# VectorE and ScalarE in source order in the gated layers, W_down's sums two steps ahead, Silu on ScalarE

## The chip, the cores and the metric

The kernel runs on one core of one Trainium2 chip. The metric is the device time of one execution in microseconds (us). Before the change the median of three runs is 2498.24 us (2491.13 to 2501.68). All arithmetic is float32.

## What is computed

Four residual layers follow each other on x of shape 32 x 64 x 1024. Cut to what matters:

```python
x = x + conv(x)                                  # a long convolution along 1024, kernel from L0's states
x = x + einsum('bsi,boi->bso', x, W1[ids1])      # one 1024 x 1024 matrix per batch row, picked by an index
x = x + einsum('bij,bkj->bik', x, W2[ids2])      # the same again
def lora(base, inp, A, B):                       # rank 16, A and B picked per batch row
    t = einsum('bri,bni->bnr', A[ids], inp)
    return base + einsum('bor,bnr->bno', B[ids], t) * 0.5
gate = lora(einsum('bnh,fh->bnf', x, W_gate), x, A_gate, B_gate)    # F = 2752 hidden columns
up   = lora(einsum('bnh,fh->bnf', x, W_up),   x, A_up,   B_up)
act  = silu(gate) * up
x = x + lora(einsum('bnf,hf->bnh', act, W_down), act, A_down, B_down)
```

## The kernel before

**Chunks and stages.** The 32 batch rows form four chunks of eight (`NCK`, 512 columns of 64 positions each). The convolution comes first, for all chunks; its result for chunks 1 to 3 waits in DRAM (`cd`). Then chunk 0's two picked matrices are applied, row by row, as sixteen "adapters": `adapter` (L275) multiplies eight 512 KB weight tiles with x, and VectorE transposes the sum and adds it (L285, L287). From there on each chunk runs `ffn`, and the adapters of the next chunk are put between its steps, where DMA loads would otherwise be few: the generator `others`, taken one at a time by `other()`.

**The gated layers.** 2560 of the hidden columns are worked through in five groups (`gi`), in three blocks: group 0, groups 1 and 2, groups 3 and 4. `gated` makes the gate product, applies Sigmoid on ScalarE and a multiplication on VectorE (L680, L681), makes the up product and multiplies (L685). The left-over columns are `rest`, three products of 7 us, in the first block. After each block W_down's product for that block is made, in steps of two column tiles, for four values of `h`.

**Fewer products by sums.** All large products use a scheme with seven products in place of eight, in which both operands are first added and subtracted (`sides`, `stationary` L430 to L433 for weights, `moving` L447 to L450 for activations) and the seven products are added afterwards. Chunk 0 (`halves`) uses one level of it, computes the weights' sums, and also stores those of a second level in DRAM (`kept`, `kept_parts`). Chunks 1 to 3 (`quarters`) use two levels and load stored sums. One `quarters` call is four `unit`s: unit (0), then (5,6), (4,3) and (1,2). In a unit TensorE makes products 0, 5, 6, 4, 1 and then two more into banks `pa`, `pb`, `pc`, `pd`; ScalarE copies `u` and `v` out (L623, L625, L635) and VectorE adds (L629, L631, L633, L639). In a unit of two, `pd` is the same bank as `pb`, and product 2 goes into it a second time, so that it waits for L633; product 3 goes into `pc` and waits for L631.

**Buffers.** All weight tiles, of adapters, gate, up and W_down, and the four tiles of stored convolution that each chunk takes over, share one ring of nine slots (`wpool`, tag "w"), filled by SP's queue in a fixed order. The sums of the weights have two slots, `up` and Sigmoid's output share one (tag "cu").[...]

**What sets the order.** TensorE's order is that of the source (`manual_schedule`). On the other engines a scheduler sets it, by priorities and estimated times, when the kernel is built; `behind(last_add)` and `behind(last_copy)` tie some work to stand behind a named instruction on its engine. Each engine then runs its list in order. W_down's step loads two tiles, makes four sums and multiplies:

```python
with behind(last_add):
    ws = stationary(wt, nt, s_tile(gpool, f"{name}_{s0}"))
for j in (0, 5, 6, 4, 1, 3, 2):
    terms = [(ws[j][:, i, :], ab[s0 - m0 + i][j]) for i in range(nt)]
```

`between(i)` is called at the end of each gate and up product: from the third on it takes an adapter, before that it brings the next chunk's x and stored convolution (`bring`) and adds the latter (`take`, L238). `moving_of(c + 1)` makes the next chunk's moving operands in the last block, all at h = 1.

Of the kernel before, what the change touches and what calls it, by code (L numbers as in the profile page):

```python
# [13 lines left out]
SP = mybir.EngineType.SP  # L14
POOL = mybir.EngineType.Pool

P = 128
# [3 lines left out]
NCK = 4  # L21
# [49 lines left out]
def kernel(  # L71
# [139 lines left out]
    last_add, last_copy = [], []  # L211

    def behind(last):
        return tc.issue_after(last[-1]) if last else ExitStack()


# [16 lines left out]
    def take(c, quarters):  # L233
        n = H // 4
        for q in quarters:
            xv = xs[c].rearrange("p k (b h) -> p (k b) h", h=H)[:, :, q * n : (q + 1) * n]
            with tc.issue_after(last_add[-1]):
                nc.vector.tensor_add(xv, xv, came.pop(q).rearrange("p i k -> p k i"))  # L238


# [56 lines left out]

    hpool = ctx.enter_context(tc.tile_pool(name="hpool", bufs=1, reuse_waits="tile"))
# [30 lines left out]
    def columns(table, c, n, name):  # L329
# [17 lines left out]
        def in_order():  # L347
            t = gpool.tile([P, n, BC, R], F32, tag="at", name=f"at_{name}", bufs=1)
            with behind(last_copy):
                nc.scalar.copy(t, raw.rearrange("p b n r -> p n b r"))  # L350
            return t.rearrange("p n b r -> p n (b r)")
# [111 lines left out]
    def halves(c, gi, g, o, xb, between):  # L463
        name = f"{c}_{gi}_{g}"
        w = (wg, wu)[g]
        lt, copy_lt = low_rank_of(c, gi, g)
        wts, sts, sides_of = [], [], []
        for m in range(MG):
            wt = []
            for i in (0, 1):  # L470
                t = wpool.tile([P, 2, KH, P], F32, tag="w", name=f"wf{i}_{name}_{m}")
                nc.sync.dma_start(t.rearrange("p k s f -> p (k s f)"), w[i, MG * gi + m])
                wt.append(t)
            wts.append(wt)

        def stationary_of(m):
            st = s_tile((gpool, qpool[0])[m], f"{name}_{m}")
            sts.append(st)
            with behind(last_add):
                sides_of.append(stationary(wts[m], KH, st))  # L480

        stationary_of(0)

        def kept(q):
# [12 lines left out]
            with behind(last_add):  # L497
                sides(a11, a12, a21, a22, *(t[:, :n, i] for i in range(4)))
# [18 lines left out]
        for m in range(MG):  # L517
# [25 lines left out]
            last_copy.append(nc.scalar.copy(v, pb).ins)  # L543
            if m == 0:
                with behind(last_copy):
                    copy_lt()
            last_add.append(nc.vector.tensor_add(u, v, u).ins)
            if m == 0:
                stationary_of(1)
                kept_parts()  # L550
            product(pc, 6, True)
            nc.vector.tensor_add(c22, pc, u)
            product(pb, 4, True)
            last_add.append(nc.vector.tensor_add(c22, pb, c22).ins)
# [4 lines left out]
            nc.vector.tensor_add(c12, pb, u)  # L559
            product(pc, 3, False)  # L560
            last_add.append(nc.vector.tensor_add(c21, pc, u).ins)
            kept(2 * m + 1)
            o_m = o[:, :, m]
            with behind(last_add):
                nc.vector.tensor_add(o_m, o_m, lt[:, :, m])
        between()

    def quarters(c, gi, g, o, xb, between):
# [26 lines left out]
        def unit(js, copies=None):  # L595
# [18 lines left out]
            banks = [ps_tile(f"pq{i}_{name}_{js_}")[:, : n * TQ] for i in range(5 - n)]  # L614
            pa, pb, pc, pd = (banks + banks[1:2])[:4]
# [5 lines left out]
            )  # L621
            product(pa, 0, True)
            nc.scalar.copy(u, pa)  # L623
            product(pb, 5, True)
            last_copy.append(nc.scalar.copy(v, pb).ins)  # L625
            if copies:
                with behind(last_copy):
                    copies()
# [4 lines left out]
            nc.vector.tensor_add(c22, pd, c22)  # L633
            product(pa, 1, False)
            nc.scalar.copy(c11, pa)  # L635
            for i in (3, 2) if n == 1 else (2, 3):
                ps, to = ((pd, c12), (pc, c21))[i - 2]
                product(ps, i, False)
                nc.vector.tensor_add(to, ps, u)  # L639
# [16 lines left out]
        (p1,) = unit((0,), copy_lt)  # L656
        nc.scalar.copy(c12, p1)
        add(c11, p1, l11)
        p6, p7 = unit((5, 6))
        add(c12, c12, p6)  # L660
        add(c21, c12, p7)
        p5, p4 = unit((4, 3))
        add(c22, c21, p5)
        add(c12, c12, p5)
        add(c21, c21, p4)
        add(c12, c12, l12)
        add(o[:, 1], o[:, 1], lt[:, 1])  # L667
        p2, p3 = unit((1, 2))
        add(c11, c11, p2)
        last_add.append(add(c12, c12, p3).ins)  # L670
        between()

    def gated(c, gi, xb, between):

        f = quarters if c else halves
        act = apool.tile([P, 2, MG, TC], F32, tag="act", name=f"act_{c}_{gi}")
        f(c, gi, 0, act, xb, lambda: between(2 * gi))
        sg = gpool.tile([P, 2, MG, TC], F32, tag="cu", name=f"sg_{c}_{gi}", bufs=1)
        for i in (0, 1):
            nc.scalar.activation(sg[:, i], act[:, i], AF.Sigmoid)  # L680
            nc.vector.tensor_mul(act[:, i], act[:, i], sg[:, i])  # L681
        up = gpool.tile([P, 2, MG, TC], F32, tag="cu", name=f"up_{c}_{gi}", bufs=1)
        f(c, gi, 1, up, xb, lambda: between(2 * gi + 1))
        for i in (0, 1):
            nc.vector.tensor_mul(act[:, i], act[:, i], up[:, i])  # L685
        return act

    def rest(c):
# [3 lines left out]
        for i in range(3):  # L692
            wt = wpool.tile([P, KT, P], F32, tag="w", name=f"wr{i}_{c}")
            nc.sync.dma_start(wt.rearrange("p k f -> p (k f)"), wr[i])
            if i == 2:
# [6 lines left out]
                nc.scalar.activation(rest1, cs[0], AF.Sigmoid)  # L702
                nc.vector.tensor_mul(rest1, rest1, cs[0])
# [22 lines left out]
        nc.scalar.activation(a[SECOND], v[SECOND], AF.Sigmoid)  # L726
        nc.vector.tensor_mul(a[SECOND], a[SECOND], v[SECOND])
# [6 lines left out]
    def prepare(c, name):  # L734

        x_c = xs[c]
        at = columns(ag if name == "g" else au, c, KT, f"{name}_{c}")()
        ps = low_rank(at, KT, lambda i: x_c[:, i, :], f"{name}_{c}")
        nc.vector.tensor_mul(tms[name], ps, bmask)

    def moving_of(c):
# [25 lines left out]
        for i in (0, 1):  # L767
            b11, b12, b21, b22 = (q_of(k, t)[i] for k in (0, 1) for t in (0, 1))
            moving(b11, b12, b21, b22, *(at_(j)[i] for j in (4, 5, 6, 3)))
            for j, q in zip(range(3), (b11, b21, b22)):  # L770
                nc.scalar.copy(at_(j)[i], q)
        b11, b12, b21, b22, t1, t2, t4 = (xd[:, :, i] for i in range(7))
        moving(b11, b12, b21, b22, t1, t2, b12, t4)
        return xd

    def ffn(c, xb, others):

        x_c = xs[c]
        ready = None

        def other():
            next(others, None)

        def between(i):

            if i > 2:
                other()
            elif c + 1 < NCK:
                if i == 1:
                    take(c + 1, (0, 1))  # L790
                if i < 2:
                    bring(c + 1, (2 * i, 2 * i + 1))
# [5 lines left out]
        for block, (m0, m1) in enumerate(BLOCKS):  # L798
# [3 lines left out]
            acts = []  # L802
            for gi in range(m0 // MG, m1 // MG):
                acts.append(gated(c, gi, xb, between))
            for _ in left:
                pass
            at = at()
            if c == 0 and last:
# [3 lines left out]
                )  # L812
            tiles = [act[:, :, m] for act in acts for m in range(MG)]
            ins = [act[:, i, :] for i in (0, 1) for act in tiles]
            if last:
# [8 lines left out]
                nc.vector.tensor_sub(wl[:, 1, 0], wl[:, 1, 0], wl[:, 1, 1])  # L824
# [3 lines left out]
            ab = []  # L828
            for i, act in enumerate(tiles):
                if i % MG == 0:  # L830
                    t3 = apool.tile([P, MG, 4, TH], F32, tag="actd", name=f"actd_{c}_{m0 + i}")
                q = [act[:, h, t * TH : (t + 1) * TH] for h in (0, 1) for t in (0, 1)]
                ab.append(moving(*q, *(t3[:, i % MG, j] for j in range(4))))

            for h in range(KH):
                name = f"{c}_{block}_{h}"
                if last and h == 1 and c + 1 < NCK:
                    ready = moving_of(c + 1)
                if last and h > 1 and c + 1 < NCK:
                    prepare(c + 1, "gu"[h - 2])  # L840
# [4 lines left out]
                for s0 in range(m0, m1, SEG):  # L845
                    nt = min(SEG, m1 - s0)
                    end = s0 + nt == m1

                    more = int(end and block == 0)
                    at_ = s0 + (block > 0)  # L850
                    wt = []
                    for i in (0, 1):
                        t = wpool.tile([P, 2, KH, P], F32, tag="w", name=f"wd{i}_{name}_{s0}")
                        nc.sync.dma_start(
                            t[:, :, : nt + more], wd[i, h, :, :, at_ : at_ + nt + more]
                        )
                        wt.append(t)
                    if more:
                        w = [t[:, 0, nt] for t in wt]
                        less = wt[0][:, 1, nt]  # L860
                        nc.vector.tensor_sub(less, *w)
                        tails = {1: (w[0], 0), 3: (w[1], 0), 4: (w[1], 1), 2: (less, 1)}
                    elif end and last:
                        w = [[wl[:, t, i, h * P : (h + 1) * P] for i in (0, 1)] for t in (0, 1)]
                        tails = {1: (w[0][0], 0), 3: (w[0][1], 0), 4: (w[1][1], 1), 2: (w[1][0], 1)}
                    with behind(last_add):
                        ws = stationary(wt, nt, s_tile(gpool, f"{name}_{s0}"))
                    for j in (0, 5, 6, 4, 1, 3, 2):
                        terms = [(ws[j][:, i, :], ab[s0 - m0 + i][j]) for i in range(nt)]
                        if end and (more or last) and j in tails:  # L870
# [505 lines left out]
```

## Time and profile before

| | |
|---|---|
| median of three runs | 2498.24 us |
| the profiled execution, whole | 2496.46 us |
| its span, first to last instruction | 2494.8 us |
| mean granted TensorE clock | 0.981 |
| convolution and chunk 0's adapters | 0 to 343 us |
| chunk 0, 1, 2, 3 of the gated layers | end near 915, 1484, 2039, 2495 us |
| one adapter on TensorE, no wait | 7.04 us |
| one W_down step of two tiles, no wait | 6.2 us |
| HBM traffic | 274 GB/s over the span |

The page names groups by source line and tile: "pq" are the banks of `quarters`, "pf" of `halves`, "po" of W_down, "pa" of the adapters; "wa" and "wb" are tiles of stored or plain weights, "wd" W_down's. A line of waits reads: engine, tile and line that waited, what released it, us in total, how often, the longest.

### The profile page before, as it was taken

How to read it: one execution, taken by the hardware profiler on the slowest of the kernel's cores; microseconds unless marked ns; L12 is line 12 of the kernel's file. 1: busy time of each engine (PE TensorE's matmuls, PEld its weight loads, DVE VectorE, ACT ScalarE, POOL GpSimd, SP SyncE). 2: the span in 40 equal slices, each digit the busy share in tenths (PEclk: the TensorE clock that was granted, in tenths of full speed). 3: DMA queues.
4: the chain of work that ended last, by engine and by line, in shares of the span. 5: the costliest groups of instructions: out<-in, count | busy, mean ns of one | idle time of the engine just before them, and what ended most of it. 6: DMA issues, size and time to landing. Idle time of an engine off the chain costs nothing.

```text
span 2494.8 us, 53575 instructions
## 1 busy us (share of the span) xinstructions
PE 2304.2 (92%) x21674; PEld 1893.0 (76%) x21674; DVE 1361.4 (55%) x2810; ACT 388.1 (16%) x848; POOL 272.0 (11%) x387
## 2 busy tenths in 40 slices
PE   5999889999999889999999999999999999989979
PEld 5986356877788677887787686887788686887878
DVE  7411148774377446655355556655356555665664
ACT  4200011110011012211022112211022112220220
POOL 4322013111022101000000101000000101000000
PEclk9999999999999889999999999999999999999999
DMA  8999986599989856589988956588988955573661
GB/s 307 355 347 376 408 339 227 207 345 357 359 324 358 267 186 227 175 305 341 358 304 326 310 187 230 180 307 328 360 301 326 313 172 178 186 243 111 238 201 64
DMA packets 232009, 688.10 MB, mean 276 GB/s; under 512 B 27458, under 2 KB 68674, under 8 KB 231250
## 3 DMA queue, kind: packets, MB, share of 16 engines
q1 hardware_dynamic: 199778, 593.66, 66.6%
q0 software_dynamic: 25184, 82.37, 9.0%
q10 hardware_dynamic: 6800, 8.65, 1.0%
q8 instruction: 171, 2.80, 0.5%
q14 instruction: 76, 0.62, 0.1%
HBM read 617.17 MB, written 67.40 MB: 274 GB/s over the span
## 4 chain that ended last, share of the span: by engine, by line
PE 69%; DVE 14%; DMA 13%; issue 3%; ACT 0%; POOL 0%; SPq 0%; POOLq 0%; DVEq 0%; ACTq 0%
PE po L875 20%; PE pq L604 19%; PE pa L275 12%; PE pf L522 8%; PE pc L1164 5%; DMA wa<-in_w 4%; DMA wa<-sums 3%; PE pr L709 3%; DMA wd<-in_wd 2%; DMA hk<-kp 2%; PE pl_d L375 1%; PE pe L404 1%; DVE t L639 1%; DMA wl<-in_bd,rows_half 1%; DVE act L667 1%
## 5 line engine op out<-in xcount | busy, mean ns | idle before, releaser
L604 PE MATMUL pq<-xd,wa 128*128 128x128 f32 x3360 | 430.1, 280 | 62.5 <-DVE t L633 47.8
L275 PE MATMUL pa<-wa,x 128*32 128x256 f32 x7872 | 459.0, 383 | 25.7 <-DMA wa<-in_w 23.6
L604 PEld LDWEIGHTS pq<-xd,wa 128*128 128x128 f32 x3360 | 403.0, 195 | 71.4 <-DVE t L633 53.6
L275 PEld LDWEIGHTS pa<-wa,x 128*32 128x32 f32 x7872 | 244.1, 110 | 226.3 <-DMA wa<-in_w 58.0
L604 PE MATMUL pq<-xd,wb 128*128 128x128 f32 x2520 | 342.4, 283 | 14.9 <-DVE t L631 13.9
L604 PEld LDWEIGHTS pq<-xd,wb 128*128 128x128 f32 x2520 | 313.7, 197 | 22.3 <-DVE t L631 16.0
L875 PE MATMUL po<-actd,s 128*128 128x256 f32 x640 | 173.0, 395 | 30.4 <-DVE s L431 30.4
L639 DVE TENSOR_TENSOR t<-pq,u 128x128 f32<-128x128 f32 (+1 forms) x240 | 93.8, 391 | 174.8 <-PE pq L604 173.0
L875 PE MATMUL po<-actd,wd 128*128 128x256 f32 x640 | 170.1, 389 | 8.7 <-DVE wd L432 7.7
L875 PE MATMUL po<-act,wd 128*128 128x256 f32 x640 | 171.2, 391 | 0.0
L430 DVE TENSOR_TENSOR s<-wd 128x256 f32<-128x256 f32 x80 | 33.6, 420 | 251.0 <-DMA wd<-in_wd 210.4
L875 PEld LDWEIGHTS po<-actd,s 128*128 128x128 f32 x640 | 125.7, 198 | 52.6 <-DVE s L431 34.8
L302 POOL DMA_INDIRECT bgu<-in_bgu,rows x44 | 53.8, 1223 | 1014.2 <-PE pe L404 934.7
L1164 PE MATMUL pc<-uf,hk 128*128 128x256 f32 (+7 forms) x1024 | 152.1, 310 | 12.1 <-DMA hk<-kp 7.5
L1164 PEld LDWEIGHTS pc<-uf,hk 128*128 128x128 f32 x1024 | 147.2, 193 | 16.4 <-issue 8.1
L522 PE MATMUL pf<-xd,wf 128*128 128x256 f32 x640 | 150.7, 381 | 0.8 <-DVE wf L432 0.8
L875 PEld LDWEIGHTS po<-actd,wd 128*128 128x128 f32 x640 | 125.1, 196 | 28.0 <-DVE wd L432 8.3
L875 PEld LDWEIGHTS po<-act,wd 128*128 128x128 f32 x640 | 119.8, 193 | 31.6 <-issue 16.0
L522 PEld LDWEIGHTS pf<-xd,wf 128*128 128x128 f32 x640 | 120.8, 190 | 18.3 <-DVE wf L432 1.2
L285 DVE STREAM_TRANSPOSE y<-pa 128x512 f32<-128x512 f32 x64 | 45.7, 714 | 154.0 <-PE pa L275 153.9
L522 PE MATMUL pf<-xd,s 128*128 128x256 f32 x480 | 113.9, 380 | 5.0 <-DVE s L431 2.8
L892 ACT COPY uo<-po 128x256 f32<-128x256 f32 x48 | 17.9, 372 | 635.7 <-PE po L875 635.6
(227 smaller groups left out, 2609.5 us busy)
## 6 DMA issues: line engine op xcount, KB each, us to landing
wa<-in_w SPq DMA_DIRECT2D x492, 512.0 KB, 7.4
wa<-sums SPq DMA_DIRECT2D x210, 512.0 KB, 5.5
wb<-parts SPq DMA_DIRECT2D x120, 384.0 KB, 5.3
wb<-in_wq SPq DMA_DIRECT2D x90, 384.0 KB, 5.2
wd<-in_wd SPq DMA_DIRECT2D x128, 256.0 KB, 4.5
hk<-kp SPq DMA_DIRECT2D x30, 1024.0 KB, 8.1
sums<-kept POOLq DMA_DIRECT2D x30, 1024.0 KB, 6.8
wd<-in_wd SPq DMA_DIRECT2D x32, 384.0 KB, 4.2
```

The lines of the kernel that those rows point to most:

```text
L275: nc.tensor.matmul(acc[i * S : (i + 1) * S, s * 256 : (s + 1) * 256], xs[c][:, kt, lo + s * S : lo + (s + 1) * S], wt[:, i * 256 : (i + 1) ...
L285: nc.vector.transpose(y, acc)
L302: nc.gpsimd.indirect_dma_start(out=t, out_offset=None, in_=table, in_offset=bass.IndirectOffsetOnAxis(ap=at_, axis=0),)
L375: nc.tensor.matmul(ps[pair(j)], at[:, i, pair(j)], x_i[:, 2 * H * j : 2 * H * (j + 1)], start=(i == 0), stop=(i == n - 1),)
L404: nc.tensor.matmul(ps[:, at_ * 2 * H : (at_ + 1) * 2 * H], bt[pair(j), g], tms[table][pair(j)], start=(g == 0), stop=True, skip_group_chec ...
L430: nc.vector.tensor_add(s1, a21, a22)
L522: nc.tensor.matmul(ps, ws[j][:, kt, :], xb[j][:, kt, :], start=start and kt == 0, stop=kt == KH - 1, skip_group_check=True,)
L604: nc.tensor.matmul(ps[:, to * TQ : (to + 1) * TQ], w[i][:, k, :], xb[:, j, SLOT[i], k, :], start=start and k == 0 and to == 0, stop=k == K ...
L639: nc.vector.tensor_add(to, ps, u)
L709: nc.tensor.matmul(ps, wt[:, kt, :], xs[c][:, kt, :], start=(kt == 0), stop=(kt == KT - 1),)
L875: nc.tensor.matmul(pss[j], *term, start=(s0 == m0 and i == 0 and home[j] % 2 == 0), stop=(end and i == len(terms) - 1), skip_group_check=True,
L1164: nc.tensor.matmul(ps[:, j, d * B :], hk[:, j, d * P : (d + 1) * P], uf[:, i + j, : KT - d, :].rearrange("p k b -> p (k b)"), start=(d == ...
```

## The change

It puts VectorE and ScalarE under the source's order from the gated layers on, and rearranges the source so that this order is a usable one.

- A list `later` holds work with a cost in us beside it. `fill(us)` runs entries from its front while they fit in `us`, `flush()` runs all. What goes there: the stored convolution's additions, now in halves, the product of act and up, and act's moving operands. The ties `behind(...)` go.
- `unit` has four banks for its products always, makes product 3 ahead of 2, and takes two amounts (or a function) for `fill`: before its first product, and after the sum of product 4.
- Silu is applied by ScalarE in place; the multiplication by Sigmoid's output goes. It stands in ScalarE's order ahead of the up product's copies.
- W_down's tiles are loaded and summed by `down_sides`, called once inside the last up product, once before the first step and then after each step's products: two steps ahead. In chunk 0 the first sums of the next `halves` call are made ahead in the same way.
- `rest`'s parts are taken after the first block's flush; the next chunk's moving operands are made in four pieces, over h = 1 to 3; the tables of its low-rank part are loaded earlier; W_down's final sums stand in another order.

```diff
+    ctx.enter_context(tc.manual_schedule(engines={DVE, ACT}))
...
+    later = deque()
+    def fill(us):
+        while later and later[0][0] <= us:
+            cost, f = later.popleft()
+            us -= cost
+            f()
+    def flush():
+        while later:
+            later.popleft()[1]()
...
     def take(c, quarters):
...
+                later.append((1.0, add))
...
-            banks = [ps_tile(f"pq{i}_{name}_{js_}")[:, : n * TQ] for i in range(5 - n)]
-            pa, pb, pc, pd = (banks + banks[1:2])[:4]
+            banks = [ps_tile(f"pq{i}_{name}_{js_}")[:, : n * TQ] for i in range(4)]
+            pa, pb, pc, pd = banks
...
+            fill(start)
             product(pa, 0, True)
...
             nc.vector.tensor_add(c22, pd, c22)
+            if callable(mid):
+                mid()
+            else:
+                fill(mid)
             product(pa, 1, False)
             nc.scalar.copy(c11, pa)
-            for i in (3, 2) if n == 1 else (2, 3):
-                ps, to = ((pd, c12), (pc, c21))[i - 2]
-                product(ps, i, False)
-                nc.vector.tensor_add(to, ps, u)
+            product(pc, 3, False)
+            nc.vector.tensor_add(c21, pc, u)
+            product(pd, 2, False)
+            nc.vector.tensor_add(c12, pd, u)
...
-        p6, p7 = unit((5, 6))
+        p6, p7 = unit((5, 6), 1.3, 1.3)
...
-        add(c12, c12, l12)
-        add(o[:, 1], o[:, 1], lt[:, 1])
-        p2, p3 = unit((1, 2))
+        p2, p3 = unit((1, 2), 0.0, lambda: add(o[:, 1], o[:, 1], lt[:, 1]))
...
-            nc.scalar.activation(sg[:, i], act[:, i], AF.Sigmoid)
-            nc.vector.tensor_mul(act[:, i], act[:, i], sg[:, i])
+            nc.scalar.activation(act[:, i], act[:, i], AF.Silu)
+        between(2 * gi)
...
+        for i in (0, 1):
+            later.append((1.2, lambda i=i: times_up(i)))
+        for m in range(MG):
+            later.append((1.7, lambda m=m: moving_act(m)))
...
+        def other(us=0.0):
+            if more_come:
+                fill(us)
+                next(others, None)
         def between(i):
             if i > 2:
-                other()
+                if i == 3:
+                    flush()
+                other(5.0)
...
+            todo = deque((h, s0) for h in range(KH) for s0 in range(m0, m1, SEG))
+            down = {}
+            def down_sides():
+                nonlocal sides0
+                if not todo:
+                    if c == 0 and not last and sides0 is None:
+                        sides0 = halves_sides(m1 // MG, 0, 0)
+                    return
+                h, s0 = todo.popleft()
...
+                for i in (0, 1):
+                    t = wpool.tile([P, 2, KH, P], F32, tag="w", name=f"wd{i}_{name}")
+                    nc.sync.dma_start(
+                        t[:, :, : nt + more], wd[i, h, :, :, at_ : at_ + nt + more]
+                    )
+                    wt.append(t)
+                ws = stationary(wt, nt, s_tile(gpool, name))
...
+                down[h, s0] = ws, tails
...
+                def behind():
+                    if end:
+                        down_sides()
+                    elif c == 0:
+                        return halves_sides(gi + 1, 0, 0)
+                act, ab_, sides0 = gated(c, gi, xb, sides0, between, behind)
...
+                if end:
+                    flush()
+                    if block:
+                        other()
+                else:
+                    between(2 * gi + 1)
+            if block == 0:
+                between(1)
+                next(left)
+                flush()
             for _ in left:
                 pass
             at = at()
+            down_sides()
...
-                if last and h == 1 and c + 1 < NCK:
-                    ready = moving_of(c + 1)
...
-                    with behind(last_add):
-                        ws = stationary(wt, nt, s_tile(gpool, f"{name}_{s0}"))
+                    ws, tails = down.pop((h, s0))
...
+                    down_sides()
                     if s0 == m0 and (block == 1 or (last and h == 0)):
                         other()
                     if h == 0 and s0 == m0:
                         tv = low_rank_down(at, ins, f"d{block}_{c}", tv, last)
+                    if s0 == m0 and last and h and more_come:
+                        steps[h]()
...
+                if last and h == KH - 1 and more_come:
+                    steps[KH]()
```

## The prediction

> **What bounds the kernel now.** I read the page's busy shares first, then the waits of TensorE over the part that the change touches (343 us, where the gated layers begin, to the end), then the timeline around its stalls, the granted clock behind them, and last the loads.
>
> ```profile
> span 2494.8 us, 53575 instructions
> PE 2304.2 (92%) x21674; PEld 1893.0 (76%) x21674; DVE 1361.4 (55%) x2810; ACT 388.1 (16%) x848; POOL 272.0 (11%) x387
> ```
> TensorE is the bound, with 190 us idle; VectorE is half empty, so it can only hurt by when it does a thing, not by how much. Before 343 us (convolution, first adapters) nothing changes, and 56 us of the idle time lie there. For the rest, "waited for: total, times, longest":
>
> ```profile
> PE pq L604 <- DVE t L633: 47.8, 30, 2.6
> PE po L875 <- DVE s L431: 30.4, 10, 7.0
> PE pq L604 <- DMA wa<-sums: 14.7, 14, 3.2
> PE pq L604 <- DVE t L631: 13.9, 11, 2.5
> PE pa L275 <- DMA wa<-in_w: 8.0, 10, 2.3
> PE po L875 <- DVE wd L432: 7.7, 1, 7.7
> ```
> With the small rest (7.2 us) this is about 130 us. The first row comes 30 times: once per `quarters` call (15 groups of three chunks, gate and up). The timeline shows how:
>
> ```profile
> 1074.16 0.68 DVE L666 TENSOR_TENSOR up<-up,lt 128x512 f32<-128x512 f32 x1
> 1074.76 1.22 DVE L667 TENSOR_TENSOR up<-up,lt 128x1024 f32<-128x1024 f32 x1
> 1075.89 0.42 DVE L629 TENSOR_TENSOR u<-u,u 128x256 f32<-128x256 f32 x1
> 1076.23 1.22 DVE L685 TENSOR_TENSOR act<-act,up 128x1024 f32<-128x1024 f32 x1
> 1077.37 0.42 DVE L631 TENSOR_TENSOR t<-pq,u 128x256 f32<-128x256 f32 x1
> 1077.89 0.42 DVE L633 TENSOR_TENSOR t<-pq,t 128x256 f32<-128x256 f32 x1
> ...
> 1078.37 1.77 PE L604 MATMUL pq<-xd,wa 128*128 128x128 f32 x8 [2.47 <-DVE t L633]
> ```
> Two 1.22 us operations that nobody waits for stand ahead of the two that free the bank TensorE wants (product 2 goes to the bank that product 4 filled). A second price follows such a stall. These are the stall and the stretch after it, as us, PE busy ..., PEclk, DMA share, GB/s:
>
> ```profile
> 1311.70:1313.80 2.10, 0.00 (x0) 0.00 (x0) 1.95 (x4) 0.37 (x1) 0.00 (x0) 1.00 0.75 300
> 1314.25:1317.66 3.41, 3.41 (x23) 2.96 (x25) 0.84 (x2) 0.00 (x0) 0.00 (x0) 0.50 0.53 181
> ```
> After a gap of two us or more TensorE often runs 3.41 us at half clock and loses half of it. I laid windows over all such stretches: 95.6 us, TensorE busy for 77.4 of them, so 38.7 us are lost beside the gaps. Last the loads, in the stretch where W_down's steps alternate with the next chunk's adapters:
>
> ```profile
> 1150.00:1263.00 113.00, 112.26 (x1350) 80.61 (x1339) 45.01 (x109) 5.04 (x13) 1.00 (x1) 1.00 0.95 347
> SPq L163 <- PE po L875: 28.2, 7, 5.7
> ```
> No stall there, but DMA is 95% busy, and SP waits for slots of the nine-slot weight ring: an adapter's eight 512 KB loads run ahead while a W_down step computes.
>
> **What the Trainium skill says.** "TensorE: Matmul & The Clock Gate", part 1, has the clock halved after an idle window of about 3413 ns; the 3.41 us stretches agree, though here gaps of 2.1 us suffice. Its "Architectural detail" calls ScalarE and VectorE strict FIFO, which is what the row of 1.22 us operations shows. "DMA: Bandwidth & Descriptors", "Anatomy of one DMA", gives a fixed cost of about 2.0 us; the shortest 512 KB landing here is 3.3 us, and at the best rate seen (417 GB/s) the bytes take 1.26, so 2.0 agrees. "ScalarE: Activation LUTs", "What ACT_TABLE_LOAD costs", gives 1283 ns per load; the trace has 1.28 us, once, for Sigmoid. Silu takes its place in the order with one load too: no change.
>
> **The change part by part**, against the profiled run's own 2496.46 us (span 2494.8; the median of runs is 2498.24, 1.8 higher).
>
> 1. Order inside `quarters`. A fourth bank, product 3 ahead of 2, the 1.22 us sum put behind the two bank-freeing sums, deferred work only where it fits. In the last unit, counted from its first product (0.89 us each): the freeing sum for product 3 ends near 3.4, needed at 4.4; the one for product 2 near 4.2, needed at 5.3; deferred pieces of up to 1.22 us ahead of the middle unit still fit. **-47.8.**
>
> 2. Gate to up without an adapter between (groups 0 and 1 of chunks 1 and 2, all five of chunk 3: 9 places). Two Silus now stand in ScalarE's queue ahead of the `u` copies that TensorE waits for. From TensorE's last product T: VectorE's two 0.69 us tail sums end at T+1.9, the Silus (Sigmoid's 1.06 each, same shape; a table function might cost 0.9 to 1.3) at T+3.9, the copy at T+4.1, where T+2.95 was wanted: 1.2, and 0.4 for the sum behind it, 1.6 where 0.99 is now. Chunk 3's only full flush between groups (after group 1, no adapter as cover): 2.3 + 2.7 us of deferred work from T+1.9, so TensorE waits from T+3.4 to T+7.5, 4.1 where 2.5 is now; after group 3 the present 2.5 goes. L631 thus goes from 13.9 to 9 x 1.6 + 4.1 = 18.5: **+4.6.**
>
> 3. W_down. Sums two steps ahead: loads have landed and VectorE's four sums are done before a step begins; the moving operands of a chunk are spread over h (now a burst; gaps of 4.42, 3.69, 3.18). L431, L432 and a stray 1.0 make 39.1. Left: chunk 3, where no adapter covers. At the end of group 2 the second sum ends at T+2.7, wanted at T+0.95: 1.7. At the end of group 4, three deferred parts stand in line and the group's first operands are ready at T+5.3: 4.4. **-33.**
>
> 4. Chunk 0's `halves`: 5.8 us of pf waits, next sums issued earlier: **-5.** Chunk starts: the x load no longer holds up two loads behind it (9.4 of the 14.7 us on sums); take 7 back, lose 3 on the rest as TensorE gets faster against DMA: **-4.**
>
> 5. Half clock: of 38.7 us I leave 10 (three chunk-3 stalls, a few others): **-28.**
>
> 6. New: the tail of a chunk. A 2.0 us subtraction stands ahead of x's last four adds, and the next chunk's first sums behind those: ready at T+5.1, wanted at T+3.4: 1.7 x 3. With the later end **+6.**
>
> 7. New: the ring. Two pairs of W_down tiles now sit in the ring while an adapter loads, four of nine slots, six while a step computes. SP's order shows it: loads 0 to 2 of an adapter find free slots, 3 and 4 take those that the running step gives back at its fifth and sixth product, 5 to 7 wait for the adapter's own first tiles. From the step's end S (a tile is used in 0.88): issues at S-1.6, -0.7, 1.1, 2.0, 2.9; at 3.4 us for the first and 1.26 apart they land at 1.9, 3.2, 4.6, 5.9, 7.2. The last is wanted at 6.2: **1.1 us per adapter.** Squeezed are six in block 1 and two in the last block, of three chunks: 24 x 1.1 = 26. The adapter ahead of each of those blocks (6) has three slots instead of five until the last unit is through: 1.65 each, 10 in all, for 6 that wait today. **+30.** Bounds per adapter: 0.3 (queues empty, 3.3 us landings overlap) to 3 (landings of 4.5 and more, as those behind other loads have).
>
> 8. Silu also takes 48 instructions and 54 us off VectorE; off the path, worth nothing alone: what would be late is still TensorE. `flush` for groups 0 is covered by 14 us of the remainder's products; sums waiting for their loads block VectorE in order, but with loads two steps early.
>
> Sum: -47.8 + 4.6 - 33 - 5 - 4 - 28 + 6 + 30 = -77, or 2419. I place the forecast a little above, at **2424**, as every gain is taken nearly whole; own range 2400 to 2445.
>
> **The rivals.**
> - *The ring costs twice as much.* Landings behind other loads took 4.5 us and more; the low DMA share I count on during the step speaks against. 30 adapters at 2.2 instead of 1.2 give +30, and some half-clock stretches stay, +8: 2457.
> - *The ring costs little,* 5 instead of 30, because the landings pipeline and the half clock goes altogether: 2419 - 25 - 8 = 2386. Against it: today's DMA there is 95% busy.
> - *The new wait wins: slower.* Place: the same 30 adapters. If an adapter's last five loads in effect start only when its own tiles come free (7.4 us is the median landing of these loads under load), it waits 4.5 us instead of 1.2, and such gaps bring half-clock stretches of 1.7 each. From 107 gained elsewhere (77 + 30), it decides from 3.6 us per adapter. At 4.5 with twenty stretches: 2496 - 107 + 135 + 34 = 2558. Against: the landing estimate above.
> - *It does not do what it says:* one fixed order on VectorE makes each sum that waits for a load or a product block all behind it, and the stalls come back elsewhere. Half of the 107 gone and the ring as costed: 2472.
>
> **How the numbers follow.** Forecast 0.55, cheap ring 0.12, dear ring 0.14, blocked order 0.10, slower 0.09. The forecast's time is the likeliest's. Range 2388 to 2475: it leaves out the slower case and part of the cheap one. About 0.5% (12.5 us) is what a measurement can tell from no change: within it lie a part of the blocked and of the slower case: faster 0.85, same 0.06, slower 0.09.
>
> **What would show it.** Right: no PE wait on t at all in the last unit (1); PE waiting for ACT's u and DVE's t for 14 us at nine places (2); W_down waits of 6 us, in chunk 3 (3); VectorE busy near 1307 (8); mean clock near 0.995 (5); PE waiting for `wa<-in_w` some 30 to 40 us in the W_down stretches, from the sixth load of an adapter on (7). Wrong: those waits at 100 us, or the L604 waits still at 40.

## The result, and the profile after

The changed kernel takes 2588.92 us (median of four runs, 2588.0 to 2595.94), the kernel before 2494.72 in the same runs: a ratio of 1.038, 95% interval 1.0348 to 1.0413. It is slower by 94 us; 2424 was forecast.

The first part of the page of the changed kernel:

```profile
span 2586.4 us, 53694 instructions
PE 2339.8 (90%) x21674; PEld 1885.9 (73%) x21674; DVE 1323.4 (51%) x2774; ACT 388.2 (15%) x848; POOL 267.6 (10%) x387
```

TensorE has the same 21674 products and 92 us more to do them in. VectorE has lost 38 us of work, which no one notices. TensorE's waits from 343 us on (what waited, what released it, us in total, times, the longest):

```profile
PE pa L293 <- DMA wa<-in_w: 92.2, 119, 3.1
PE pl_u L393 <- ACT at_u L368: 22.0, 3, 7.3
PE pl_g L393 <- ACT at_g L368: 22.0, 3, 7.3
PE pq L621 <- ACT u L641: 16.6, 12, 2.4
PE pr L745 <- DMA wr<-in_wr: 9.6, 2, 4.9
PE pq L621 <- DMA wa<-sums: 7.2, 12, 1.1
PE pq L621 <- DVE t L648: 7.0, 16, 4.3
PE po L958 <- DVE actd L466: 4.1, 2, 3.3
PE po L958 <- DVE s L449: 1.8, 1, 1.8
```

The two large rows of before are gone: `pq` waits no more for the sum that frees its bank (47.8 us, L633), and `po` waits 5.9 us in all where it waited 39.1. In their place stand the adapters' loads (8.0 before), two rows of waits for ScalarE that did not exist, and `wr`, the weights of the remainder.

TensorE's order is the same in both kernels, save for products inside a unit, so its matmuls can be laid side by side. For each one the time since the start of the one ahead of it was taken in both traces; the differences, summed by the tile that is written:

```
adapters (pa)                       +123.2 us
low-rank products (pl_g, pl_u)       +53.6
remainder, chunk starts (pr)         +15.0
gate and up, chunks 1 to 3 (pq)      -63.1
W_down (po)                          -40.3
gate and up, chunk 0 (pf)             -4.6
the rest                              +3.8
from 343 us to the end               +87.7
```

This counts waits and half clock together (half clock: stretches in which TensorE is granted half of its clock). The gains are 108 us. Three losses of 192 us stand against them, and each has its own place.

*ScalarE's queue.* The timeline of the changed kernel (start, us, engine, line, what; in brackets the idle time before it and what ended it; "..." marks lines left out), in chunk 2's last block at the end of h = 1:

```profile
2106.33 1.03 PE L958 MATMUL po<-act,s 128*128 128x256 f32 x4
2107.39 0.42 DVE L448 TENSOR_TENSOR s<-wd 128x256 f32<-128x256 f32 x1 [3.68 <-PE po L958]
...
2108.87 0.42 DVE L980 TENSOR_TENSOR x<-po,x 128x256 f32<-128x256 f32 x1
...
2112.32 0.42 DVE L992 TENSOR_TENSOR x<-x,uo 128x256 f32<-128x256 f32 x1
2112.43 0.82 ACTq L996 DMA_DIRECT2D out_y<-x  x2
2113.58 1.04 ACT L368 COPY at_g<-raw_g 128x1024 f32<-128x1024 f32 x1 [11.80 <-DVE x L992]
2114.53 1.65 ACT L806 COPY xd<-x 128x512 f32<-128x512 f32 x3
```

ScalarE issues the DMA that stores `out_y`. In source order that issue stands ahead of the copy of `at_g`, and it waits for VectorE's last addition to x, the end of fifteen operations that themselves start when TensorE is done. The copy needs none of it: the last of `raw_g` had been issued at 2051.9 us and landed at 2060.2, 53 us ahead of the copy. TensorE's next product needs the copy and stands still for 7.32 us; then it runs its 64 products at half clock, as the windows over the stall and the stretch after it show (us, PE busy ..., PEclk, DMA share, GB/s):

```profile
2106.50:2114.60 8.10, 0.86 (x4) 0.40 (x3) 5.27 (x15) 1.02 (x2) 0.00 (x0) 0.68 0.41 136
2114.70:2118.30 3.60, 3.60 (x65) 2.99 (x65) 0.00 (x0) 1.49 (x3) 2.61 (x5) 0.50 0.24 77
```

It happens six times, for g and u in three chunks: 44 us of waits. In the kernel before, the scheduler had put the copy ahead of the store, and no such wait exists. The Trainium skill, "Perfetto Trace Analysis", section "DMA Instruction — HWDGE (DVE, Sync)", draws a DMA instruction's semaphore wait in the issuing engine's own sequencer, for VectorE and SyncE as issuers; the trace shows the same of ScalarE: the copy starts 1.15 us after the store is let go, though its own data had long been there.

*The ring.* One adapter between two W_down steps of the changed kernel, on TensorE:

```profile
1242.96 3.66 PE L293 MATMUL pa<-wa,x 128*32 128x256 f32 x64
1247.03 1.07 PE L293 MATMUL pa<-wa,x 128*32 128x256 f32 x16 [0.42 <-DMA wa<-in_w]
1248.30 1.07 PE L293 MATMUL pa<-wa,x 128*32 128x256 f32 x16 [0.20 <-DMA wa<-in_w]
1250.18 1.07 PE L293 MATMUL pa<-wa,x 128*32 128x256 f32 x16 [0.81 <-DMA wa<-in_w]
1251.52 1.07 PE L293 MATMUL pa<-wa,x 128*32 128x256 f32 x16 [0.26 <-DMA wa<-in_w]
```

Four tiles (64 products) are there, the other four come one by one. Counted from the step's end S (1242.9), SP issued the last five loads at S-1.6, S-0.7, S+1.1, S+2.0 and S+2.9, exactly where the prediction had them. Its waits in the W_down stretch of chunk 1 (1195 to 1316 us) say why no earlier:

```profile
SPq L166 <- PE pa L293: 32.8, 41, 1.9
SPq L166 <- PE po L958: 28.1, 14, 4.5
```

SP waits up to 4.5 us for a product of the running step to give back a slot, then for the adapter's own. Meanwhile the queues run dry (in the microsecond from 1241 us nothing was moved): the same stretch was at a DMA share of 0.95 and 347 GB/s before, and now is at

```profile
1195.00:1316.00 121.00, 107.13 (x1223) 67.84 (x1224) 37.44 (x88) 1.12 (x3) 1.61 (x3) 0.97 0.84 299
```

*The chunk starts.* `wr` is loaded behind the first W_down pair and waits for slots with it: two waits of 4.7 to 4.9 us.

TensorE runs at half clock for 110.3 us of busy time after 343 us, where it was 77.4: by half of that, some 16.5 us more are lost beside the gaps.

### The profile page after: what moved, and what is told of

Read it like the earlier page. It is cut to its first block, busy times and chain, and to the rows that moved or that the text cites. A ratio compares the mean times of both kernels' runs of the same rounds, so it can differ in the third digit from the quotient of the medians.

```text
span 2586.4 us, 53694 instructions
## 1 busy us (share of the span) xinstructions
PE 2339.8 (90%) x21674; PEld 1885.9 (73%) x21674; DVE 1323.4 (51%) x2774; ACT 388.2 (15%) x848; POOL 267.6 (10%) x387
## 4 chain that ended last, share of the span: by engine, by line
PE 66%; DMA 17%; issue 9%; DVE 5%; ACT 1%; POOL 1%; POOLq 1%; SPq 0%; ACTq 0%; DVEq 0%
PE pq L621 23%; PE po L958 19%; DMA wa<-in_w 11%; PE pa L293 7%; PE pf L537 7%; PE pc L1255 5%; DMA wa<-sums 3%; PE pr L745 3%; DMA hk<-kp 1%; PE pl_d L393 1%; ACT act L704 1%; PE pe L422 1%; DMA wr<-in_wr 0%; POOLq L355 0%; PE pl_g L393 0%
## 5 line engine op out<-in xcount | busy, mean ns | idle before, releaser
L293 PE MATMUL pa<-wa,x 128*32 128x256 f32 x7872 | 502.2, 393 | 109.1 <-DMA wa<-in_w 106.1
L293 PEld LDWEIGHTS pa<-wa,x 128*32 128x32 f32 x7872 | 238.4, 112 | 353.8 <-DMA wa<-in_w 202.8
L621 PE MATMUL pq<-xd,wa 128*128 128x128 f32 x3360 | 419.7, 276 | 7.6 <-DMA wa<-sums 7.2
L621 PEld LDWEIGHTS pq<-xd,wa 128*128 128x128 f32 x3360 | 397.2, 193 | 10.4 <-DMA wa<-sums 7.7
L621 PE MATMUL pq<-xd,wb 128*128 128x128 f32 x2520 | 334.0, 280 | 23.6 <-ACT u L641 16.6
L621 PEld LDWEIGHTS pq<-xd,wb 128*128 128x128 f32 x2520 | 306.5, 194 | 32.6 <-ACT u L641 18.8
L958 PE MATMUL po<-act,wd 128*128 128x256 f32 x640 | 174.8, 397 | 0.0
L958 PE MATMUL po<-actd,s 128*128 128x256 f32 x640 | 167.4, 384 | 5.9 <-DVE actd L466 4.1
L958 PE MATMUL po<-actd,wd 128*128 128x256 f32 x640 | 165.2, 381 | 0.0
L958 PEld LDWEIGHTS po<-act,wd 128*128 128x128 f32 x640 | 121.2, 196 | 34.3 <-issue 19.3
L958 PEld LDWEIGHTS po<-actd,s 128*128 128x128 f32 x640 | 123.6, 194 | 24.6 <-DVE actd L466 4.9
L958 PEld LDWEIGHTS po<-actd,wd 128*128 128x128 f32 x640 | 122.6, 192 | 17.0
L537 PEld LDWEIGHTS pf<-xd,s 128*128 128x128 f32 x480 | 91.0, 190 | 14.1 <-issue 1.8
```

Of the source, the lines that this page charges most:

```text
L293: nc.tensor.matmul(acc[i * S : (i + 1) * S, s * 256 : (s + 1) * 256], xs[c][:, kt, lo + s * S : lo + (s + 1) * S], wt[:, i * 256 : (i + 1) ...
L537: nc.tensor.matmul(ps, ws[j][:, kt, :], xb[j][:, kt, :], start=start and kt == 0, stop=kt == KH - 1, skip_group_check=True,)
L621: nc.tensor.matmul(ps[:, to * TQ : (to + 1) * TQ], w[i][:, k, :], xb[:, j, SLOT[i], k, :], start=start and k == 0 and to == 0, stop=k == K ...
L958: nc.tensor.matmul(pss[j], *term, start=(s0 == m0 and i == 0 and home[j] % 2 == 0), stop=(end and i == len(terms) - 1), skip_group_check=True,
```

## The experiments

**Each loss alone.** Three edits, each to the changed kernel (in edited kernels a line can stand some lines lower: L625 and L977 are then L621 and L958). First (e1) the loads and sums of the step after next go behind the adapter, wherever one follows the step (`waits`):

```diff
-                    down_sides()
+                    if not waits:
+                        down_sides()
                     if s0 == m0 and (block == 1 or (last and h == 0)):
                         other()
+                        if waits:
+                            down_sides()
```

with the same behind the adapter at the end of an h.

> The changed kernel, with one thing moved: where an adapter follows a step of the W_down block, the loads and sums of the step after next come behind the adapter instead of ahead of it, so that while a step runs four of the nine slots hold W_down tiles and not six. Theory 'ring' (W_down's tiles hold the slots that the adapter's loads need, and the loads stop until a step ends): five of an adapter's eight tiles are then on their way at its start instead of three; the adapters, which take 123 us more than in the kernel before, fall back to within 30 us of it, the waits for wa<-in_w go from 92 us to under 25, and the time from 2589 to 2475-2500 us. Rival 'transfers' (the loads come late because other transfers run beside them now, not for want of a slot): the waits stay over 70 us and the time within 20 us of 2589.

2519.45 us (2510.9 to 2524.89), 69 us less; beside the kernel before still 1.009 (1.0065 to 1.0115). In the stretch that the windows showed above, shifted to where it now lies, the queues are full again:

```profile
1170.00:1274.00 104.00, 99.86 (x1220) 67.80 (x1220) 36.43 (x87) 1.12 (x3) 1.61 (x3) 1.00 0.96 344
```

and an adapter there has seven tiles at its start and waits once:

```profile
1225.55 6.47 PE L293 MATMUL pa<-wa,x 128*32 128x256 f32 x112
1232.24 1.07 PE L293 MATMUL pa<-wa,x 128*32 128x256 f32 x16 [0.23 <-DMA wa<-in_w]
```

The 1220 or so products of that stretch took 121 us and now take 104, with the same loads, so other transfers beside the loads are not the cause; with SP's waits above, the slots are. The 27 adapters behind W_down steps took 80 us more than in the kernel before and now take 14. But the time is above the expected band, and the waits for wa<-in_w are 47.4 us: the expectation had counted all 123 us to this place. Of the 123, 24 belong to the six adapters ahead of a W_down block and 17 to five in chunk 0's gates. This edit does not touch them, and they still take 26 and 17 more.

Second (e2), the two copies:

```diff
+                if last and h in (1, 2) and more_come:
+                    at_next = tables.pop()()
                 nc.scalar.copy(u1, p1)
```

with `at_next` handed to `prepare`.

> The changed kernel, with two ScalarE copies moved: at_g and at_u (the columns that pl_g and pl_u are multiplied with) are copied ahead of the copy of p1 at the end of the W_down half before, and so no longer stand behind the issue of out_y, which waits for VectorE's last addition to x. Theory 'ScalarE's queue': the six waits of 7.3 us before pl_g and pl_u go (44 us), and with them 9 to 10 us that these 384 matmuls lose at half clock; the time falls by 50 to 54 us to 2535-2540. Rival 'the wait is inherited' (behind the copy the raw columns' transfer or the additions to x are late too): under 15 us are gained.

2523.48 us (2520.57 to 2528.28), 65 us less where 50 to 54 were expected, ratio 1.0104 (1.0077 to 1.013). The waits before `pl_g` and `pl_u` are gone but for one of 1.2 us. Laid side by side these products take 53.6 us less, as expected. The busy time at half clock falls from 110.3 to 64.4 us, by more than those products had of it; that is enough for the rest.

Third (e3), `wr` ahead of the first W_down pair in chunks 1 to 3:

```diff
                     if end:
-                        down_sides()
+                        if block or c == 0:
+                            down_sides()
...
                 next(left)
+                if c:
+                    down_sides()
                 flush()
```

> The changed kernel, with the first W_down loads of chunks 1 to 3 issued behind wr's first tile instead of ahead of all three. Theory 'ring at the chunk start': the two waits of 4.8 us for wr go, with their half clock 10 to 15 us; 2574-2580. Rival 'x is late there': the wait moves to another operand of pr and the time stays within 5 us.

2574.17 us (2569.51 to 2580.16), 14.7 less; the wait for `wr` falls to 0.6 us. Laid side by side, `pr` takes 14.8 us less, and `pq` gives 5.6 back: TensorE comes to the stored sums' loads earlier than they do.

**All three together (e5).**

> The changed kernel with the three edits of the first runs together: W_down's loads and sums behind the adapter, the two at copies ahead of the copy of p1, wr ahead of the first W_down loads. Theory 'three separate causes': their gains (69, 65 and 15 us) add up: 2435-2450. Rival 'one debt of transfers' (each edit let the DMA queues catch up, so that the second one gains less): 2460-2480.

2451.23 us (2443.52 to 2461.95), ratio 0.984 (0.9801 to 0.9878): 138 us less than the changed kernel, of a sum of 149, and just above the expected band. They are nearly separate causes, and with them mended the change is a gain, of 1.6%. The waits for wa<-in_w are at 49.2 us, as in e1; nothing else is over 17.

**The bank order.** The kernel before with the four banks and product 3 ahead of 2, nothing else (e4):

```diff
-            banks = [ps_tile(f"pq{i}_{name}_{js_}")[:, : n * TQ] for i in range(5 - n)]
-            pa, pb, pc, pd = (banks + banks[1:2])[:4]
+            banks = [ps_tile(f"pq{i}_{name}_{js_}")[:, : n * TQ] for i in range(4)]
+            pa, pb, pc, pd = banks
...
-            for i in (3, 2) if n == 1 else (2, 3):
+            for i in (3, 2):
```

> The kernel before, with one part of the change alone: each unit of quarters has four banks, and its product 3 comes ahead of product 2. Step 1 of the prediction (the 47.8 us that pq waits for t go with the banks, and some 15 us of half clock with them): 2425-2440. Rival (VectorE, in its scheduler's order, is then late at the next addition): some of it comes back as waits at L631's addition, 2460-2490.

2483.93 us (2475.49 to 2489.27), ratio 0.9937 (0.991 to 0.9964): 17 us and not 60, as the rival expected. Its waits for t:

```profile
PE pq L604 <- DVE t L631: 45.1, 41, 2.5
PE pq L604 <- DVE t L633: 0.8, 1, 0.8
```

L633 is freed of its 47.8 us, and L631 has gone from 13.9 to 45.1. At the place of the prediction's timeline both sums still stand behind the same two 1.22 us operations (at 1073.25 and 1074.72 us here), and TensorE waits 1.59 us for the first sum where it waited 2.47 for the second: the bank changed which of the two it waits for. The reverse (e8) is the changed kernel with the old banks and product order, the minus lines of this diff in place of the plus lines:

> The changed kernel, with the banks and the order of products in quarters as in the kernel before (three banks in units of two, product 2 ahead of 3). Theory 'banks and order share it' (the banks alone took 32 us from pq in the kernel before, and what pq gains in the changed kernel is 63): 25 to 40 us more than 2589. Rival, the prediction's step 1 (the banks carry it all): 55 to 70 us more. Rival 'order alone' (with VectorE's order written out the old banks are freed in time): within 10 us of 2589.

2581.76 us (2581.42 to 2586.15), ratio 1.0359 (1.0336 to 1.0382), not to be told from the changed kernel's 1.038. Its `pq` waits are

```profile
PE pq L621 <- ACT u L641: 16.7, 13, 2.3
PE pq L621 <- DVE t L648: 6.9, 16, 4.3
```

the same as with four banks. VectorE's new list does it without the fourth bank: its freeing sums come early, and three banks suffice.

**Silu.** The changed kernel with Sigmoid and VectorE's product again (e11), here and in the two places of `rest`:

```diff
-            nc.scalar.activation(act[:, i], act[:, i], AF.Silu)
+            nc.scalar.activation(sg[:, i], act[:, i], AF.Sigmoid)
+            nc.vector.tensor_mul(act[:, i], act[:, i], sg[:, i])
```

> The changed kernel with Sigmoid on ScalarE and the product on VectorE in place of Silu, all else as in the changed kernel. The prediction's step 8 (Silu brings nothing by itself): within 8 us of 2589; VectorE's busy time rises by some 50 us. Rival (VectorE's two products of 1.2 us stand ahead of the sum of u and v in the up half's first unit, and PE waits for them): 10 to 30 us above 2589.

2604.38 us (2600.43 to 2610.2), 15 more; the intervals of the two ratios just overlap (1.0397 to 1.0471 here), but the traces laid side by side give 16 us too, with 20 more on `pq`. The wait of `pq` for ScalarE's u stays at 16.2 us, that for t at L648 goes from 7.0 to 16.0, VectorE's busy time from 1323.4 to 1374.7. In source order the two products stand ahead of the first sum of the up product, where TensorE waits for them. ScalarE's time is the same, 1.05 us for Silu as for Sigmoid on 128 x 1024.

**What is left of the ring.** The kernel with the three edits, and added to them (e6) the same rule for all other adapters: whatever shares the ring is loaded behind the adapter's eighth tile, its sums ahead of the adapter's transpose (a function that `adapter` calls between its last product and the transpose):

```diff
+        while hooks:
+            hooks.popleft()()
         y = ypool.tile([P, 512], F32, tag="y", name=f"y{layer}_{b}")
```

> The kernel of e5 with the same rule for the other adapters: in chunk 0 the W_gate and W_up tiles of the next half, and in all chunks the first W_down tiles of blocks 1 and 2, are loaded behind the adapter's eight tiles, and their sums are made ahead of the adapter's transpose. Theory 'ring': what adapters still cost in e1 beside the kernel before (9 adapters in chunk 0's gates 34 us, the adapter ahead of the W_down block 4 to 5 us in four places of chunks 1 and 2) goes: 40 to 50 us off e5, 2385-2405. Rival: the tiles that now come later are late for their own sums, and PE waits for s (pf, po) instead: over 20 us of such waits, and under 25 us off e5.

2441.55 us (2435.92 to 2446.45), only 10 less, which is the rival's figure. Both theories held, each in its place: adapters take 35 us less than in the run before it, and chunk 0's gate adapters are at 7.04 us exactly; W_down takes 25 us more, over half of it in chunk 3, where no adapter comes and the edit had put the first sums behind the products with up:

```profile
PE pa L293 <- DMA wa<-in_w: 24.5, 42, 3.4
PE po L972 <- DVE s L451: 22.5, 8, 10.0
```

The two Silus of a group behind the copies of u and v (e7), and, added to that, chunk 3's first sums ahead again (e9):

```diff
             nc.scalar.copy(v, pb)
+            while silus:
+                silus.popleft()()
...
-                    if end and block == 0 and c == 0:
+                    if end and (not more_come if block else c == 0):
                         down_sides()
...
-                        other(0.0, down_sides)
+                        other(0.0, down_sides if more_come else None)
```

> The kernel of e6, with the two Silus of a group behind the copies of u and v of the up half's first unit instead of ahead of them on ScalarE. Theory: the 16.6 us that pq waits for u at L641 (12 places) go: 12 to 18 us off e6. Rival: ScalarE's copies were late for another reason, or the wait moves to t: under 6 us off e6.

> The kernel of e7, with the first W_down sums of blocks 1 and 2 in chunk 3, where no adapter comes, made ahead of the products with up and the moving sides again, as in the changed kernel. Theory (the 7.2 and 10.0 us that po waits for s in chunk 3 of e7 come from that place alone): 15 to 22 us off e7, 2404-2412. Rival (VectorE's backlog there is the same in any order): under 5 us off e7.

2426.41 us (2419.26 to 2428.89) and 2406.99 us (2401.75 to 2418.35): 15 and 19 less, both as expected. The wait for u falls from 16.7 to 7.0 us. Last (e10), one step ahead where adapters are:

```diff
-            down_sides()
+            if not (block and more_come):
+                down_sides()
...
-                        other()
-                        if waits:
-                            down_sides()
+                        other(0.0, down_sides if waits else None)
```

> The kernel of e9, with the W_down tiles one step ahead in place of two wherever an adapter follows the step, loaded behind the adapter's eight tiles, with their sums ahead of its transpose. Theory 'ring, no more is to be had' (five of eight tiles on their way already keep the queues full, and the sums of a tile that comes behind the adapter are made too late): the waits for wa<-in_w fall from 25 to under 15 us, the waits of po for s rise by over 15 us, and the time is 0 to 15 us above e9. Rival 'seven slots as in the kernel before': 10 to 20 us below e9.

2396.03 us (2395.15 to 2397.17), ratio 0.9598 (0.9567 to 0.9629), the lowest of all. The first theory was wrong that five preloaded tiles were enough: with two W_down tiles fewer in the ring the adapters wait 10.9 us where they waited 23.4 in e9, and `po` waits 19.7 us in all where it waited 12.1; its waits for s rose by 4 us, not 15. The median is 11 us below e9's, as the rival had it, but the two intervals just meet (e9's ratio is 0.9617 to 0.9695), and in the two traces, where the adapters take 19 us less and W_down 8 more, only 4 us of it are left after 343 us. Its page and its waits:

```profile
span 2394.0 us, 53748 instructions
PE 2277.3 (95%) x21674; PEld 1875.1 (78%) x21674; DVE 1323.5 (55%) x2774; ACT 386.3 (16%) x848; POOL 267.9 (11%) x387
```

```profile
PE pa L293 <- DMA wa<-in_w: 10.9, 17, 1.7
PE po L977 <- DVE s L451: 9.3, 7, 1.9
PE pq L625 <- DMA wa<-sums: 7.9, 14, 1.2
PE pq L625 <- ACT u L645: 7.0, 3, 2.4
```

Laid beside the kernel before, its `pq` are 75.7 us shorter, `po` 26.5, and adapters 1.6 longer. The same kernel with the old banks (e12):

> The kernel of e10 with the banks and the order of products in quarters as in the kernel before. Theory 'order alone' (e8: with VectorE in source order the old banks are freed in time, and the banks were not what removed the 47.8 us): within 8 us of e10's 2396, and no wait of pq for c22's addition over 5 us in all. Rival (in e8 the other waits hid it; with TensorE 95% busy the three banks cost again): 15 to 40 us above e10.

2403.1 us (2400.85 to 2413.55), ratio 0.9616 (0.9588 to 0.9643). The median is 7 us above e10's and the intervals of the ratios overlap, but all seven runs lie above e10's four: the fourth bank may be worth a few us here, far from the 47.8. No wait for c22's addition came back: t is waited for 5.2 us in all, of which 4.3 are one wait in chunk 3 that both have. A row that e10 does not have is the price of the shared bank, where product 4 waits until ScalarE has copied v out of it:

```profile
PE pq L625 <- ACT u L647: 5.5, 10, 0.6
```

## Why the prediction was wrong

The side was wrong, and steps 6 and 7 are where. By its own steps:

1. *Order inside `quarters`, -47.8.* The amount came, for another reason than the first one named. The row is gone, but the fourth bank is not why: alone it brought 17 us (e4), and without it the row does not come back (e8, e12). Product 3 ahead of 2 went in and out with the bank. Of what the step listed, that leaves the place of the 1.22 us sum and of the deferred work; no run changes these two alone.
2. *Silu ahead of the copies, L631's 13.9 to 18.5.* 16.6 us for u, at 12 places where nine were counted, and 7.0 for t: 23.6, 5 us more than expected. The single flush in chunk 3 was put at 4.1 us and took 4.3.
3. *W_down, 6 us left.* 5.9 left: 4.1 and 1.8, in the two places named.
4. *Chunk 0 and chunk starts, -9.* `pf` waits 1.1 us, as expected, and the stored sums 7.2 instead of 14.7, a little better. But the step overlooked that `wr` now stands behind the first W_down pair: +15 (e3).
5. *Half clock, 10 us left.* 55 us were left (half of 110.3), as the new stalls bring it back; the side-by-side figures of steps 6 and 7 contain their part of it. The mean clock given as a sign was 0.995, and 0.971 came. In e10 it is 18 us (half of 36.1).
6. *The tail of a chunk, +6.* This step failed. It followed VectorE's list to x's last additions and asked when the next chunk's remainder would get x. It did not go through ScalarE's list, where the store of `out_y` waits for the same additions, with the copies of `at_g` and `at_u` behind it. The waits are six times 7.3 us; with their half clock they cost 54 us side by side and 65 in e2, where nothing was expected. The delay that the step priced, the next chunk's first sums, did not show: with the copies and `wr` in time (e5) `pr` waits 0.2 us in all.
7. *The ring, +30.* This step failed by its size. The place and the issue times were right; the cost was +123. The first term at fault is the landing. It was taken as 3.4 us for a first load and 1.26 more for each next. In the adapter shown above the last four loads took 4.8, 4.2, 5.2 and 5.7 us from issue to use and came 1.27 to 1.88 us apart, the last at S+8.6 and not at S+7.2. The 1.26 is 512 KB at 417 GB/s, the best slice of a trace. From 1243 to 1252 us the queues were 0.99 busy and moved 350 GB/s, which is 1.5 us per tile; the prediction's own stretch before, 0.95 busy at 347 GB/s, had shown that rate. The 2.0 us fixed cost of the Trainium skill, "DMA: Bandwidth & Descriptors", "Anatomy of one DMA", on which the step leaned, is given there for DMAs that GpSimd issues; these are SP's, and the measurement decides. So an adapter behind a step cost 3.0 us (80 over 27) where the step put 1.1; 3 was its upper bound. The six ahead of a block cost 4.1 each, not 1.65. The second term at fault is the count: the five adapters in chunk 0's gates, 3.5 us each, meet W_gate's and W_up's tiles in the ring in the same way (with those behind them, in e6, they take 7.04 us), and were not counted.
8. *Silu by itself, nothing.* It is worth some 15 us (e11): half idle as VectorE is, in a fixed order its 1.2 us products stand where TensorE waits. VectorE's busy time, expected near 1307, came to 1323.4; Silu's part of it is 51 us (e11), near the 54 of the step.

The slower rival named the right place, and put its turning point at 3.6 us per adapter over thirty of them, 108 us. The ring passed that by number more than by price: 123 us over 38 adapters, 3.2 each. It did not decide alone: with only W_down's steps mended (e1), or only ScalarE's copies (e2), the kernel is still 0.9% and 1.0% slower than before; with all of it mended (e10, which also moves the Silus) it is 4% faster, at 2396.

Of the signs listed, "those waits at 100 us" was the one for wrong, and 92.2 came.

## What to carry to other kernels

When an engine is put into source order, go through its whole list, the DMAs that it issues among them: each instruction that waits holds up all behind it, and the price is paid by whoever waits for those. When a buffer is filled further ahead, count what else draws on the same slots, and ask whether the transfers there had time to spare. Here the queues were 95% busy before and had next to none: with slots lacking, the same products took 121 us and not 104. Loads that can wait belong behind those that cannot, in the order of need.

## What the runs showed of the hardware

Half clock goes by how busy TensorE was in a fixed stretch of time, not by the length of one gap. In all fourteen traces after 343 us, the half clock begins and ends on a grid of 3.413 us. Of the stretches of this grid at full clock, all 199 in which TensorE was busy for less than 1.47 us were followed by one at half clock, and none of the 8148 in which it was busy for more than 1.87 us; between the two, some were and some were not. So a gap of 2.1 us counts if it falls into one stretch, as in the prediction's example (the half clock begins at 1314.25 us, and the gap from 1311.7 to 1313.8 lies within the 3.41 us before, in which TensorE was busy for 1.29 us), and short gaps add up: in the changed kernel the half clock at 1198, 1266 and 1898 us follows strings of waits between adapter tiles of which the longest is 1.45, 1.65 and 1.90 us. The stretch ahead of 1198 us and the one after it (windows as above):

```profile
1194.71:1198.12 3.41, 1.41 (x28) 0.51 (x24) 3.38 (x6) 0.00 (x0) 1.60 (x3) 1.00 0.99 368
1198.12:1201.53 3.41, 3.41 (x36) 1.49 (x40) 1.53 (x5) 0.00 (x0) 0.01 (x1) 0.50 1.04 362
```

512 KB loads into queues that had just run dry took 4.2 to 5.7 us until their use, where the shortest landing seen before was 3.3. And the order alone is worth this much: e10 and the changed kernel hold the same 21674 matmuls and read and write the same bytes, in another order on VectorE, ScalarE and SP's queue, and their spans are 2394.0 and 2586.4 us.
